# A two-layer graph network kernel: fewer copied source tiles, a second table kept on chip, node steps one group apart, one-hot matrices of 80 nodes

## The chip, the cores and the metric

One core of a Trainium2 chip runs the whole program. The metric is the device time of one execution in microseconds; the kernel before was run three times (3557.40, 3561.74 and 3564.12 us, median 3561.74 us), and once more under the profiler. "POOL" is GpSimd, "DVE" VectorE, "ACT" ScalarE, "PE" TensorE and "SP" SyncE in all that follows.

## What is computed

12,500 nodes of 128 features each, and 200,000 edges, sorted by target node. Two layers follow each other, each with a normalisation in front and a residual around it:

```python
h = relu(layernorm(x))
agg = segment_sum(h[src], dst)                       # layer 0
x = x + agg @ W_rel.T + b_rel + h @ W_root.T
h = relu(layernorm(x))
w = silu(edge_attr @ We1 + be1) @ We2 + be2          # layer 1
agg = segment_sum(h[src] * w, dst)
x = x + h + silu(agg @ Wn1 + bn1) @ Wn2 + bn2
```

What costs time is the row lookup `h[src]`: 200,000 rows of 512 bytes per layer, at indices in no order. All data are float32.

## The kernel before

**Groups and tiles.** The edges are cut into tiles of 128 and groups of 8 tiles (1,024 edges): 196 groups, 1,563 tiles per layer, the last group with three tiles. A group's eight tiles of source rows sit in one of six buffers `hs` (`HB`). The nodes are cut into 25 batches of 512 (the last of 212).

**A tile of source rows, way one: gather.** `fetch` (L241 to L257) issues one indirect DMA per tile on POOL's queue: 128 rows from HBM by a column of `src_sb`. Layer 0 reads `x` itself for the first `FG` groups (29, L134), and normalises those rows on chip (`norm`, L311); from then on it reads `h0_d`, the normalised nodes that `node_first` (L418) wrote out meanwhile, one batch per group. Layer 1 reads `h1_d`. Ahead of a group POOL waits until the group that had the buffer six groups earlier has been scattered (L244), once for the last batches of `h0_d` and once for the last two batches of `h1_d`.

**Way two: copy.** The node features of a layer also lie transposed on chip, feature by partition and node by column, in `table`. For the groups in `helped` (L67) the last tile is not gathered: DVE and ACT copy its 128 columns one by one from `table` into `hc` (`put`, L578, 128x4 bytes each; DVE takes the first 60 columns in layer 0 and 56 in layer 1, ACT the others), with the column numbers loaded into registers 16 at a time (`take`, L566); PE turns the tile back (`turn`, L608) and ACT puts it into `hs` (`place`, L614). `fetch` then issues seven gathers in place of eight. `HELP` (L35) says how many: one tile in every group of layer 0 from group 30 on, nine tiles in ten groups of layer 1 from group 26 on, each used `HW` = 4 groups after it was copied. That is 160 and 147 tiles.

**Sum by target.** For each tile DVE builds a one-hot matrix (`compare`, L259): 128 edges by `W` = 128 nodes counted from the group's first target. PE multiplies rows by one-hot (`scatter`, L368, eight matmuls into one bank), and DVE adds the window of `W` columns into `agg` (`add`, L384), where sums are kept transposed. A check on the indices sends the program to a slow second version of itself (L791 on) if some edge lies outside its group's window.

**Layer 1's edge weights.** `load` brings the edge features, `hidden` (L334) and `weigh` (L346) run both matmuls, DVE adds the bias and multiplies the rows.

**Node steps.** When the groups that can touch a batch are done, layer 0 runs `node_sum`, `node_norm`, `node_keep` and `node_store` (L452 to L501) in four successive groups: root and neighbour matmuls, moments, deviations, a clearing of that part of `agg`, normalisation, the sum that layer 1's end needs (`keep_d`), and the stores. Layer 1's table is made in its first 25 groups: `node_again` (L503) loads each batch of `h1_d` back on SP's queue, `node_turn` (L511) turns it on PE and ACT copies it into `table`, over layer 0's table. So layer 1's copied tiles start at group 26.

**Order.** All engines are programmed by hand in one static order (L745 to L784): for each group `fetch` of the next one, `compare`, the normalisation in the first groups, `add` of the group before, `scatter`, then what `plan` (L706) has put beside the group, then `spread` (the copies). Semaphores are waited for by `at` (L227), which makes the engine's own queue stand.

Of the kernel before, what the change touches and what calls it, by code (L numbers as in the profile page):

```python
# [11 lines left out]
I32 = mybir.dt.int32  # L12
# [11 lines left out]
W = 128  # L24
# [10 lines left out]
HELP = ((1, 1), (9, 10))  # L35
# [31 lines left out]
def helped(n_nodes, n_edges):  # L67

    ng = n_edges // GE
    nbt = len(last_groups(n_nodes, n_edges))
    layers = []
    for begin, (tiles, groups) in ((min(ng, nbt + FB) + 1, HELP[0]), (nbt + 1, HELP[1])):
        ends = (begin - 1 - -(i + 1) * groups // tiles for i in range(ng * tiles // groups))
        layers.append((begin, [(e + HW, e) for e in ends if e + HW < ng - 1]))
    return layers

# [12 lines left out]
def kernel(  # L92
# [41 lines left out]
    FG = min(NG, NBT + FB)  # L134
    helps = [
        (layer, h, e, begin, j)
        for layer, (begin, groups) in enumerate(helped(N, n_edges))
        for j, (h, e) in enumerate(groups)
    ]
    helped_groups = {(layer, h) for layer, h, *_ in helps}  # L140
# [17 lines left out]
    table = single([P, -(-N // P) * P], "table")  # L158
    agg = single([P, NW * WG], "agg")
    keep = table.rearrange("p (t d) -> p t d", d=D)  # L160
    table_b = table.bitcast(U8)
# [15 lines left out]
    with (  # L177
# [13 lines left out]
        hid = many(2, [P, GT * P], "hid")  # L191
        st, mv = many(2, [P, NB, 6], "st"), many(2, [P, NB, 2], "mv")
# [6 lines left out]
        help_i, = many(1, list(help_t.shape), "help_i", I32)  # L199
# [41 lines left out]
        def fetch(layer, g):  # L241

            k = layer * NG + g
            at(G, done["src", 0 if g < 8 else 1], done.get(("ap", k - (HB if g < NG - 8 else LB))))  # L244
            if layer:
                at(G, *(done["h1 out", b] for b in range(max(0, NBT - 2), NBT)))
            elif g >= FG:
                at(G, *(done["h0 out", b] for b in range(max(0, NBT - 3), NBT)))
            for t in range(tiles_of[g] - ((layer, g) in helped_groups)):
                ins = G.indirect_dma_start(  # L250
                    out=hs[k % HB][:, t, :], out_offset=None,
                    in_=h1_d if layer else x if g < FG else h0_d,
                    in_offset=bass.IndirectOffsetOnAxis(
                        ap=src_sb[:, g * GT + t : g * GT + t + 1], axis=0
                    ),
                )
                done["hs", k] = inc(ins, f"hs{k % HB}", 16)  # L257
# [12 lines left out]
        def stats(xr, n, rows, st_, mv_, sd_, free):  # L270

            at(V, *free)
            for t in range(n):
                ins = V.bn_stats(st_[:rows, t, :], xr[:rows, t, :])  # L274
            at(V, inc(ins, "dve"))
            for t in range(n):
                ins = V.bn_aggr(mv_[:rows, t, :], st_[:rows, t, :])  # L277
            at(A, inc(ins, "dve"))
            ins = A.activation(sd_[:rows, :n], mv_[:rows, :n, 1], AF.Sqrt, bias=eps[:rows])  # L279
            return inc(ins, "act")  # L280

        def scales(n, rows, mv_, sd_, rs_, nm_, deviations):
            at(V, deviations)
            ins = V.reciprocal(rs_[:rows, :n], sd_[:rows, :n])
            at(V, inc(ins, "dve"))
            ins = V.scalar_tensor_tensor(
                nm_[:rows, :n], mv_[:rows, :n, 0], -1.0, rs_[:rows, :n], op0=ALU.mult, op1=ALU.mult
            )
            return inc(ins, "dve")
# [44 lines left out]
        def hidden(g):  # L334
# [7 lines left out]
            at(A, done["hp", g], done.get(("wp", g - 2)))  # L342
# [41 lines left out]
        def add(layer, g):  # L384
# [7 lines left out]
            at(V, done["ap", k], done.get(("add", k - 1)), done["agg"])  # L392
            window = agg[:, ds(firsts[k - g % GL][g % GL], W)]
# [51 lines left out]
        def node_table(b, turned):  # L445
            n0, nt = batches[b]
            m = nt * P
            at(A, done["turned", b])
            ins = A.copy(table[:, n0 : n0 + m], turned.rearrange("p t d -> p (t d)")[:, :m])  # L449
            done["table", b] = inc(ins, "act")  # L450

        def node_sum(b):  # L452

            n0, nt = batches[b]
            at(T, done.get(("keep", b - 1)), done["const"], done["ones"], done["table", b])
            T.matmul(op[:, :nt, :], ones_r, b_rel_r[:, :nt, :], start=True, stop=False)
            for layer_agg, w_sb in ((table, w_root_sb), (agg, w_rel_sb)):
                for t in range(nt):
                    s = n0 + t * P
                    ins = T.matmul(  # L460
                        op[:, t, :], layer_agg[:, s : s + P], w_sb,
                        start=False, stop=(layer_agg is agg and t == nt - 1),
                    )
                at(T, done["add", ready[b]])
            done["op", b] = inc(ins, "pe")
            at(V, done["op", b], done["xt", b])
            o = op[:, :nt, :]
            ins = V.tensor_add(o, o, xt[b % XB][:, :nt, :])  # L468
            done["dev", b] = stats(
                op, nt, P, stn[2], mvn[2], sdn[2], (inc(ins, "dve"), done.get(("h1", b - 1)))  # L470
            )
            ins = V.memset(agg[:, n0 : n0 + nt * P], 0.0)
            done["agg"] = inc(ins, "dve")

        def node_norm(b):
            n0, nt = batches[b]
            at(A, scales(nt, P, mvn[2], sdn[2], rsn[2], nmn[2], done["dev", b]))
            if b < 2:
                at(A, *(done["h0 out", b] for b in range(max(0, NBT - 3), NBT)))
            else:  # L480
                at(A, done["h1 out", b - 2], done["keep", b - 2])
# [20 lines left out]

        def node_again(b):  # L503

            i = b % 3
            at(S, done["h1 out", b], done.get(("turned again", b - 3)))
            if b < 3:
                at(S, *(done["h1 out", c] for c in range(max(0, NBT - 2), NBT)))
            done["h1 in", b] = node_dma(b, h0[i], h1_d, f"h1in{i}", True)

        def node_turn(b):  # L511

            n0, nt = batches[b]
            at(T, done["h1 in", b], done["b3"])
            for t in range(nt):
                ins = T.transpose(op[:, t, :], h0[b % 3][:, t, :], ident)  # L516
            done["turned", b] = done["turned again", b] = inc(ins, "pe")
            at(A, done["op", NBT - 1], *done.get("columns", ()))
            node_table(b, op)
            done["b3"] = done["table", b]  # L520

        def node_hidden(b):
# [3 lines left out]
            ins = T.matmul(b3[:, :m], wn1_sb, agg[:, n0 : n0 + m], start=True, stop=True)  # L526
# [39 lines left out]
        def take(engine, chunk):  # L566
# [4 lines left out]
            _, places = nc.values_load_multi_w_load_instructions(  # L571
                help_at[i % P : i % P + 1, i // P, lo:hi], engines=[kind],
                min_val=TABLE, max_val=TABLE + 4 * (N - 1),
                skip_runtime_bounds_check_because="sources are nodes",
            )
            return chunk, places

        def put(engine, taken):  # L578

            (i, lo, hi), places = taken  # L580
            at(engine, done.get(("tile", i - 3)), *(done["table", b] for b in range(NBT)))
            for c, place_ in zip(range(lo, hi), places):
                to, column = hc_b[i % 3][:, 4 * c : 4 * c + 4], table_b[:, ds(place_ - TABLE, 4)]
# [7 lines left out]
        def spread(layer, g):  # L591
# [4 lines left out]
            for engine, rest in ((V, hooks), (A, list(chunks(layer, g, A)))):  # L596
                for chunk in rest or (chunks(layer, g, V) if engine is V and not layer else ()):
# [16 lines left out]
        def place(i, layer, h):  # L614
# [3 lines left out]
            done["hx", k] = done["placed", i] = inc(A.copy(hs[k % HB][:, GT - 1, :], bank), "act")  # L618
# [3 lines left out]
        with tc.tile_critical():  # L622
# [32 lines left out]
            done["agg"] = inc(A.copy(agg, zero.to_broadcast([P, NW * WG])), "act")  # L655
# [9 lines left out]
            ins = V.tensor_scalar(help_at, help_i, 4.0, float(TABLE), op0=ALU.mult, op1=ALU.add)  # L665
# [42 lines left out]

            for layer, parts in (
                (0, (node_sum, node_norm, node_keep, node_store)),  # L710
                (1, (node_hidden, node_out, node_out_store)),
            ):
                begin = 0 if layer else FG
                for b in range(NBT):
                    begin = max(begin, ready[b] + 1)
                    for i, part in enumerate(parts):
                        plan(layer, begin + i, lambda b=b, part=part: part(b))
                    begin += len(parts) - 1
            for b in range(min(XB, NBT)):
                plan(0, NBT + 1, lambda b=b: node_load(b))  # L720
            for b in range(NBT):
                plan(1, b - 1, lambda b=b: node_again(b))
                plan(1, b, lambda b=b: node_turn(b))
            for b in range(min(2, NBT)):
                plan(1, ready[0] - 1, lambda b=b: node_load(b, keep_d))
            for i, (layer, h, e, begin, j) in enumerate(helps):
# [6 lines left out]
                if not layer:  # L733
                    plan(0, e + 2, lambda i=i, h=h: place(i, 0, h))
            placed = {e + 1: (i, 1, h) for i, (layer, h, e, *_) in enumerate(helps) if layer}
# [8 lines left out]
            for layer in range(2):  # L744
# [5 lines left out]
                for g in range(NG):  # L750
# [3 lines left out]
                    if not layer:  # L754
                        if g + 1 < NG:
                            compared = compare(0, g + 1)
                            if not g:
                                done["oh", 1] = inc(compared, "dve")
                        if g < FG:
                            for c in range(-(-tiles_of[g] // NB)):  # L760
                                push(norm(g, c))
                            push(node_first(g) if g < NBT else nothing)
# [17 lines left out]
                    if layer and g in placed:  # L780
                        place(*placed[g])
# [193 lines left out]
```

## Time and profile before

| | |
|---|---|
| three runs | 3557.40, 3561.74, 3564.12 us |
| profiled execution | 3553.55 us |
| its span, first to last instruction | 3551.7 us |
| gathers on POOL | 2,819 (232 from `x`, 2,587 from `h0_d` or `h1_d`), 944 ns each |
| copied columns | 17,832 on DVE at 150 ns, 21,464 on ACT at 190 ns |
| one-hot builds on DVE, 128x1024 | 392, 475.0 us |
| scatter matmuls on PE, 128x128 | 6,252 records (two per tile), 1214.2 us |
| busy: PE, DVE, ACT, POOL | 64%, 71%, 74%, 75% |
| granted TensorE clock, mean | 0.753 |

Busy time counts what the profile has as an instruction's duration. Register loads, waits and the time between two DMA issues are not in it, so an engine that is shown at 75% may still be one that never rests: what tells the two apart is the list of what it waited for. "issue" as a releaser means that the engine waited for nothing that the profile shows. The profiled execution was 8.2 us below the median of the three runs, 0.2%.

### The profile page before, as it was taken

To read this page: it belongs to the slowest core of one execution; us is meant where nothing else is said; L and a number is where in the kernel's file an instruction comes from. 1 tells how busy PE (TensorE), PEld (TensorE's weight loads), DVE (VectorE), ACT (ScalarE), POOL (GpSimd) and SP (SyncE) were. 2 spreads that over 40 slices of the span, in tenths; PEclk is the share of its full clock that TensorE was granted. 3 is DMA by queue.
4 is the path that set the end of the run, shared out by engine and by line. 5 is a ranking of instruction groups with operands and counts; after the bars stand their busy time and mean duration, and the time that the engine had idled before them with its cause. 6 is when DMAs were issued, how large, how long until landed. Compare 5 with 4: busy or idle time off the path is not lost.

```text
span 3551.7 us, 73201 instructions
## 1 busy us (share of the span) xinstructions
PE 2286.8 (64%) x11405; PEld 1833.0 (52%) x11405; DVE 2510.7 (71%) x20197; ACT 2620.0 (74%) x22584; POOL 2662.7 (75%) x2826
## 2 busy tenths in 40 slices
PE   3444455445454454455567778878888788888887
PEld 3443444444444444444456566656566566566565
DVE  5555777676766767776433378888888888888885
ACT  6554888788878878887511278987888789888984
POOL 7777777777777777777677777777777777777776
PEclk7566656666666667656678888898888888988988
DMA  4332322222222222222233333332332233333322
GB/s 123 106 96 74 83 69 63 63 66 69 63 63 68 66 63 66 69 61 60 84 105 105 95 82 86 88 85 79 87 89 83 81 87 90 84 83 86 87 82 62
DMA packets 201107, 284.08 MB, mean 80 GB/s; under 512 B 49305, under 2 KB 150260, under 8 KB 195620
## 3 DMA queue, kind: packets, MB, share of 16 engines
q0 software_dynamic: 90208, 184.93, 20.0%
q1 hardware_dynamic: 110214, 94.30, 8.7%
q14 instruction: 396, 3.24, 0.3%
q8 instruction: 93, 1.52, 0.2%
q10 hardware_dynamic: 196, 0.09, 0.0%
HBM read 253.52 MB, written 25.60 MB: 79 GB/s over the span
## 4 chain that ended last, share of the span: by engine, by line
POOL 59%; issue 20%; PE 9%; DVE 5%; DMA 5%; ACT 2%; DVEq 0%; ACTq 0%; POOLq 0%; SPq 0%
POOL hs L250 59%; DMA hs<-h_d,src_sb 5%; PE bank L376 4%; PE pair L353 2%; ACT hc L587 2%; DVE hc L585 2%; DVE hs L365 2%; PE pair L340 1%; DVE pair L361 1%; PE bank L460 0%; DVE oh L263 0%; PE bank L526 0%; DVEq L571 0%; DVE xt L545 0%; ACTq L571 0%
## 5 line engine op out<-in xcount | busy, mean ns | idle before, releaser
L250 POOL DMA_INDIRECT hs<-h_d,src_sb x2587 | 2442.5, 944 | 798.5 <-issue 776.6
L587 ACT COPY hc<-table 128x4 uint8 x21464 | 2135.3, 190 | 63.3 <-issue 52.1
L376 PE MATMUL bank<-oh,hs 128*128 128x128 f32 x6252 | 1214.2, 373 | 671.7 <-DVE hs L365 300.2
L376 PEld LDWEIGHTS bank<-oh,hs 128*128 128x128 f32 x6252 | 1127.2, 279 | 885.1 <-DVE hs L365 435.4
L585 DVE TENSOR_TENSOR hc<-table,bank 128x4 uint8<-128x4 uint8 x17832 | 1303.1, 150 | 282.6 <-issue 274.7
L263 DVE TENSOR_TENSOR oh<-bank,rel 128x1024 f32<-128x1024 f32 x392 | 475.0, 1212 | 0.1
L353 PE MATMUL pair<-we_sb,hid 128*128 128x128 f32 x3126 | 428.7, 296 | 3.4 <-DVE xt L488 3.4
L361 DVE TENSOR_TENSOR pair<-pair,be_sb 128x1024 f32<-128x1024 f32 x196 | 240.2, 1226 | 261.1 <-PE pair L353 260.8
L353 PEld LDWEIGHTS pair<-we_sb,hid 128*128 128x128 f32 x3126 | 418.5, 215 | 3.5 <-DVE xt L488 3.5
L340 PE MATMUL pair<-ef,we_sb 50*128 50x512 f32 (+1 forms) x782 | 409.3, 645 | 1.2 <-ACT hid L343 1.2
L365 DVE TENSOR_TENSOR hs<-pair,hs 128x1024 f32<-128x1024 f32 x196 | 239.4, 1221 | 163.5 <-DMA hs<-h_d,src_sb 151.8
L612 PE MATMUL pair<-ident,hc 128*128 128x128 f32 x160 | 64.1, 401 | 434.6 <-ACT hc L587 277.2
L343 ACT ACTIVATE hid<-pair,be_sb 128x1024 f32<-128x1024 f32 x196 | 216.9, 1107 | 106.8 <-PE pair L340 106.3
L250 POOL DMA_INDIRECT hs<-in_x,src_sb x232 | 219.0, 944 | 71.2 <-issue 70.4
L612 PEld LDWEIGHTS pair<-ident,hc 128*128 128x128 f32 x160 | 28.7, 180 | 460.1 <-issue 141.1
L340 PEld LDWEIGHTS pair<-ef,we_sb 50*128 50x128 f32 x782 | 135.0, 192 | 132.7 <-issue 120.2
L279 ACT ACTIVATE sdn<-mvn,eps 128x4 f32<-128x4 f32 (+1 forms) x50 | 14.5, 289 | 247.0 <-DVE mvn L277 247.0
L449 ACT COPY table<-bank 128x512 f32<-128x512 f32 (+1 forms) x25 | 14.4, 577 | 176.2 <-PE bank L516 176.2
L528 ACT ACTIVATE hid<-bank,bn_sb 128x512 f32<-128x512 f32 (+1 forms) x25 | 17.0, 678 | 153.9 <-PE bank L526 153.9
L274 DVE BATCH_NORM_STATS2 st<-hs 128x6 f32<-128x128 f32 x232 | 50.3, 279 | 111.2 <-DMA hs<-in_x,src_sb 111.2
L394 DVE TENSOR_TENSOR agg<-agg,bank 128x128 f32 x392 | 109.2, 279 | 27.0 <-PE bank L376 19.7
L468 DVE TENSOR_TENSOR bank<-bank,xt 128x512 f32<-128x512 f32 (+1 forms) x25 | 17.2, 688 | 149.4 <-PE bank L460 149.4
(68 smaller groups left out, 910.4 us busy)
## 6 DMA issues: line engine op xcount, KB each, us to landing
hs<-h_d,src_sb POOLq DMA_INDIRECT x2587
ef<-in_ef_t SPq DMA_DIRECT2D x98, 408.0 KB
xt<-in_x SPq DMA_DIRECT2D x48, 256.0 KB, 3.9
h_d<-h SPq DMA_DIRECT2D x48, 256.0 KB, 2.5
keep_d<-xt SPq DMA_DIRECT2D x24, 256.0 KB, 2.4
h<-h_d SPq DMA_DIRECT2D x24, 256.0 KB, 5.3
xt<-keep_d SPq DMA_DIRECT2D x24, 256.0 KB, 10.0
out_x<-xt SPq DMA_DIRECT2D x24, 256.0 KB, 2.7
```

The lines of the kernel that those rows point to most:

```text
L250: ins = G.indirect_dma_start(out=hs[k % HB][:, t, :], out_offset=None, in_=h1_d if layer else x if g < FG else h0_d, in_offset=bass.Indire ...
L263: return V.tensor_tensor(oh[k % OB][:, :n, :], io.unsqueeze(1).to_broadcast([P, n, W]), rel[:, g, :n].unsqueeze(2).to_broadcast([P, n, W]) ...
L340: ins = T.matmul(hp_b[:, c : c + m], we1_sb, e[:, c : c + m], start=True, stop=True)
L343: ins = A.activation(hid[g % 2][:, :n], hp_b[:, :n], AF.Silu, bias=be1_sb)
L353: ins = T.matmul(wp[:, t, :], hid[g % 2][:, t * P : (t + 1) * P], we2_sb, start=True, stop=True)
L361: ins = V.tensor_add(w, w, be2_sb.unsqueeze(1).to_broadcast([P, n, D]))
L365: done["msg", g] = inc(V.tensor_mul(h, w, h), "dve")
L376: ins = T.matmul(ap[k % AB], hs[k % HB][:, t, :], oh[k % OB][:, t, :], start=(t == 0), stop=(t == tiles_of[g] - 1),)
L394: done["add", k] = inc(V.tensor_add(window, window, ap[k % AB]), "dve")
L585: ins = V.tensor_tensor(to, column, zero_b, ALU.bitwise_or)
L587: ins = A.copy(to, column)
L612: done["tile", i] = inc(T.transpose(bank, hc[i % 3], ident), "pe")
```

## The change

- `HELP` becomes three tiles in four groups in layer 0 and three in five in layer 1. Layer 0's copies begin at group 18 (`FG` is 17 now) and layer 1's at group 1. The number of tiles is 129 and 113.
- `node_first` runs twice per group, so layer 0's table and `h0_d` are complete after 13 groups in place of 25.
- `table` and `agg` become two halves of one tensor that change roles: layer 0 has its table in the first half and its sums in the second; each batch, once normalised, is turned on PE and copied by ACT over its own sums (`node_turn`, `node_send`), where it is layer 1's table. Layer 1 sums into the first half, which is cleared by four ACT copies in groups 191 to 194 and two DVE memsets. `node_again`, with its loads of `h1_d`, is gone.
- The node steps of layer 0 are seven, each planned one group after the one it waits for; near the layer's end they are drawn together by a factor of three.
- `W` is 80: one-hot matrices, scatter matmuls and window adds are 80 nodes wide.
- In layer 0 the first register load for DVE's copies is taken right after `compare`.

```diff
-W = 128
+W = 80
-HELP = ((1, 1), (9, 10))
+HELP = ((3, 4), (3, 5))
...
-    for begin, (tiles, groups) in ((min(ng, nbt + FB) + 1, HELP[0]), (nbt + 1, HELP[1])):
+    for begin, (tiles, groups) in ((min(ng, -(-nbt // 2) + FB) + 1, HELP[0]), (1, HELP[1])):
...
-    FG = min(NG, NBT + FB)
+    FG = min(NG, -(-NBT // 2) + FB)
...
+    both = single([P, 2 * NW * WG], "both")
+    halves = both[:, : NW * WG], both[:, NW * WG :]
+    agg = halves[1]
...
-            for t in range(tiles_of[g] - ((layer, g) in helped_groups)):
+            for t in range(tiles_of[g] - helped_groups.count((layer, g))):
...
-            at(T, done.get(("keep", b - 1)), done["const"], done["ones"], done["table", b])
+            at(T, done.get(("sent", b - 1)), done["const"], done["ones"], done["table", b])
...
-            ins = V.memset(agg[:, n0 : n0 + nt * P], 0.0)
-            done["agg"] = inc(ins, "dve")
+            if b >= cleared:
+                at(V, done["op", b], *done.get("columns", ()))
+                ins = V.memset(halves[0][:, n0 : n0 + WG], 0.0)
+                done["sums", 1].append(inc(ins, "dve"))
+
+        def clear(b0, b1):
+
+            at(A, done["op", b1 - 1], *done.get("columns", ()))
+            s0, s1 = b0 * WG, b1 * WG
+            ins = A.copy(halves[0][:, s0:s1], zero.to_broadcast([P, s1 - s0]))
+            done["sums", 1].append(inc(ins, "act"))
...
-            done["h1 in", b] = node_dma(b, h0[i], h1_d, f"h1in{i}", True)
...
-            at(T, done["h1 in", b], done["b3"])
+            at(T, done["h1", b], done["keep", b])
             for t in range(nt):
-                ins = T.transpose(op[:, t, :], h0[b % 3][:, t, :], ident)
+                ins = T.transpose(op[:, t, :], h1[b % 2][:, t, :], ident)
+            done["h1 turned", b] = inc(ins, "pe")
+
+        def node_send(b):
+            n0, nt = batches[b]
+            at(A, done["h1 turned", b])
+            ins = A.copy(halves[1][:, n0 : n0 + nt * P], b3[:, : nt * P])
+            done["sent", b] = done["b3"] = inc(ins, "act")
...
-                (0, (node_sum, node_norm, node_keep, node_store)),
+                (0, (
+                    (0, node_sum), (1, node_moments), (2, node_deviations), (3, node_scales),
+                    (4, node_norm), (5, node_keep), (5, node_store), (5, node_turn), (6, node_send),
+                )),
...
+                        if not layer and begin > NG - 9:
+                            i //= 3
...
+                        hooks.extend(chunks(0, g, V))
                         if g + 1 < NG:
                             compared = compare(0, g + 1)
+                            hook()
...
                         if g < FG:
+                            if 2 * g < NBT:
+                                push(node_first(2 * g))
                             for c in range(-(-tiles_of[g] // NB)):
                                 push(norm(g, c))
-                            push(node_first(g) if g < NBT else nothing)
+                            push(node_first(2 * g + 1) if 2 * g + 1 < NBT else nothing)
```

## The prediction

> **What bounds the kernel now.** I read the page's busy shares and its chain first, then what POOL waited for, then the work by stage. The shares do not name a bound: four engines are between 64% and 75%. The chain does.
>
> ```profile
> ## 4 chain that ended last, share of the span: by engine, by line
> POOL 59%; issue 20%; PE 9%; DVE 5%; DMA 5%; ACT 2%; DVEq 0%; ACTq 0%; POOLq 0%; SPq 0%
> ```
>
> POOL's gathers and the "issue" time between them are 79% of it. Whether POOL is the bound all the way is decided by its waits:
>
> ```profile
> POOL hs L250 <- issue: 847.0, 2779, 0.3
> POOL hs L250 <- DMA h_d<-h: 10.3, 1, 10.3
> POOL hs L250 <- PE pair L340: 3.4, 11, 0.3
> POOL hs L250 <- PE bank L376: 2.7, 9, 0.3
> ```
>
> The columns are total us, times, longest. The 0.3 us before a gather is there 2,779 times for nothing visible, and the few that carry a name are no longer: this is the price of one gather after another, not a wait. One wait of 10.3 us, at the switch of layers, is the only time that POOL stands for others. So 2,819 gathers go out one after another, and the end comes when the last is done. Their pace, from the timeline: layer 1's first gather starts at 1766.10 us and its last, the 1,416th, at 3532.49, so 1766.39 / 1415 = 1.248 us each (944 ns busy, 0.30 between). Layer 0, 4.47 to 1754.86 in 1,401 steps, gives 1.249. The sum 1,403 x 1.249 + 10.0 + 1,416 x 1.248, with 3.1 us ahead and 18.3 us behind (3533.4 to 3551.7), is 3551 us, which is the span.
>
> Does this pace depend on what the other engines do? The work by stage answers it, a stretch without copies against one with them:
>
> ```profile
> core 0: us, PE busy (x) PEld busy (x) DVE busy (x) ACT busy (x) POOL busy (x), PEclk, DMA share, GB/s
> ...
> 1800.00:1900.00 100.00, 75.95 (x412) 59.38 (x412) 38.46 (x41) 17.16 (x21) 75.62 (x81) 0.82 0.40 108
> ...
> 2400.00:2800.00 400.00, 330.30 (x1735) 246.91 (x1734) 332.59 (x2451) 343.00 (x3008) 302.23 (x321) 0.87 0.30 84
> ```
>
> DVE goes from 38% to 83%, ACT from 17% to 86%, DMA from 40% to 30%, and POOL is at 75.6% in both. It neither waits for DVE and ACT nor is slowed by them.
>
> **The change, part by part.**
>
> *Number of copied tiles.* In the built programs POOL issues 2,819 gathers before and 2,884 after (136 from `x`, 2,748 from `h0_d` and `h1_d`). The earlier starts add groups to the copying, and the lower rates take more away: 160 + 147 = 307 tiles become 129 + 113 = 242. 65 more gathers x 1.2486 us = +81.2 us, all of it on the path, as POOL has no idle time to put them in.
>
> *Copies saved.* DVE loses 17,832 - (129x60 + 113x56 = 14,068) = 3,764 columns x 150 ns = 565 us, ACT 21,464 - 16,908 = 4,556 x 190 ns = 866 us. By the stage rows above this is beside POOL: 0. One rule speaks for a gain: the Trainium skill, "SBUF — State Buffer", in its warning on DVE blocking a DMA, says that DVE instructions in a two-port mode lock GpSimd out of writing descriptors. If each copy held POOL for its 150 ns, up to 565 us would come back. The row disagrees: 2,451 DVE instructions per 400 us against 41 per 100 leave POOL's share equal to 0.06 points, so at most 0.08% of the span, 3 us; I take 0. (The page names one-input instructions outside that mode as harmless; no row here shows the mode.)
>
> *One-hot of 80 nodes.* The builds of 128x384 took 0.49 and 0.55 us, those of 128x1024 1.21, so about 0.78 for 640: 392 x 0.43 = 169 us less on DVE, and PE and the window adds shrink too. Beside POOL: 0, except at the two ends, where the last scatter (0.94 and 0.83 us) and the window add (0.28) lie on the path. Between nothing and five eighths, some 0.3 to 0.5 us at each: I take -0.8 in all. The inputs' widest group reaches 71 nodes past its first target, so no edge falls out of a window of 80, and the slow version does not run.
>
> *Tables sooner.* Each of the first 13 groups gets a second batch on DVE and ACT. In the stretch from 50 to 250 us, 20 groups, ACT is busy 66.2 + 11.6 us with rows and 32.9 + 11.2 + 5.6 with batches: 3.9 + 2.5 = 6.4 us per group. A second batch makes it 8.9, and POOL's pace gives 8 x 1.249 = 9.99. So ACT has 1.1 us to spare where it had 3.6. What covers a shortfall: the new wait, for `h0_d` before group 17, comes at 3 + 136 x 1.249 = 173 us. The 25th batch belongs to group 12, whose rows land by some 135 us; with a group's work and the store (2.5 us to landing) it is out by about 150. The slack is some 23 us over 13 groups, so POOL waits only if a group takes over 11.8 us. Queued behind that wait are all of layer 0's gathers from group 17. Bounds: 0; and, if ACT's waits for DVE's moments (83.3 us in these 20 groups, 4.2 each) stayed whole, 13.1 us a group and 13 x 3.1 - 23 = 17 us. I take 0: those waits sit in time that was spare, and shrink when more is queued.
>
> *Table of layer 1 from layer 0.* 25 loads leave SP's queue and 98 turns and 25 copies (0.58 us) move from layer 1 to layer 0. No gather waits for any of it: 0. Each is planned after what it needs, so PE, which stands for `keep` at a turn with the next `scatter` behind it, finds it done; POOL would notice only a PE six groups (50 to 60 us) late, three in the last eight groups.
>
> *Node steps a group apart.* ACT's 247.0 us of waiting for moments (17.0 at most) and DVE's 149.4 for `node_sum` go away. They hide behind POOL: 0. It matters at the switch of layers, where the last batch has no later group:
>
> ```profile
> 1754.86 0.94 POOL L250 DMA_INDIRECT hs<-h_d,src_sb  x1 [0.30 <-issue]
> ...
> 1760.57 0.43 DVE L468 TENSOR_TENSOR bank<-bank,xt 128x256 f32<-128x256 f32 x1 [1.33 <-PE bank L460]
> ...
> 1763.40 0.34 SPq L411 DMA_DIRECT2D h_d<-h  x1
> ...
> 1766.10 0.94 POOL L250 DMA_INDIRECT hs<-h_d,src_sb  x1 [10.30 <-DMA h_d<-h]
> ```
>
> Landing, scatter, add, sum, moments, sqrt, scales, normalisation, store and its landing are the same steps after: 10 us stay. The DVE memset in it is 512 wide in place of 256 (0.48 for 0.27, partly beside the sqrt): +0.1. The batch before is done earlier, and had not been what ended last.
>
> *Early register load in layer 0, clearing by ACT* (four copies, 12,800 columns took 10.86 us, so about 10 in all): hidden by the same cover, 0.
>
> **Sum.** +81.2 - 0.8 + 0.1 = +80.5 us. On the profiled execution, 3553.55 + 80.5 = 3634; on the median of the runs, 8.2 us higher, 3642. I predict for the median: 3642 us, 2.3% slower.
>
> **Rivals.**
> 1. *POOL waits as well.* ACT falls behind in the first 13 groups and the wait at group 17 shows, or PE is held at a turn near the end of layer 0, where only three buffers cover it. For: ACT at 8.9 of 10.0 us, and a turn holds PE for a normalisation (1.50), a sum (0.68) and the turn (0.60) if nothing was ahead, 3 us for each of the last two batches. Against: 23 us of slack. Up to 17 + 6 = 23 us more: 3643 to 3665, say 3655. Chance 0.12.
> 2. *Faster: POOL is freed.* DVE's copies do hold back the descriptors, in the copying stages of both layers. Each gather must become 81 / 2884 = 28 ns quicker before this pays; at the lock's full price, 565 us, the time would be 3642 - 565 = 3077, and it decides from a seventh of that price. Against: the equal shares above. Chance 0.02.
> 3. *No difference: the copies were the bound.* ACT at 86% with register loads on top would set the pace, POOL's 0.3 us would be back-pressure, and the lighter load would pay for the gathers: 3562. Against: the same 0.3 us at 1800 to 1900 us, where nothing is copied, and at the very start. Chance 0.02.
>
> That leaves 0.84 for the forecast. A measurement of this kernel can tell about 0.2% from no change. Slower by over 0.2%: 0.84 + 0.12 = 0.96; within: 0.02; faster: 0.02. The range: the profiled execution and the runs span 3553.55 to 3564.12, which with +80.5 is 3634 to 3645; 5 us below for a pace that is 1.6 ns quicker per gather, and up to the first rival's 3665. So 3629 to 3665.
>
> **What would show it.** In the profile after: 2,884 gathers at 944 ns with 0.30 between, POOL's busy share still 75 to 77% in every slice, a span near 3632. DVE busy near 49% ((2510.7 - 565 - 169) / 3632) and ACT near 48% ((2620.0 - 866) / 3632), with no gain from it. One wait of about 10 us at the switch; a second one, before the first gather from `h0_d`, would be the first rival. A gather mean below 916 ns or gaps below 0.27 us would be the second. It is wrong if POOL's idle time has another named releaser, or if the pace differs from 1.248 us.

## The result

The changed kernel took 3652.64 us (median of four runs, 3647.13 to 3652.77), the kernel before 3561.46 us (3557.40 to 3564.12): a ratio of 1.0253, with a 95% interval of 1.0235 to 1.0271. The difference is 91.2 us where 80.5 was predicted. The profiled execution took 3652.66 us, its span is 3650.9 us.

The chain that ended last, after:

```profile
## 4 chain that ended last, share of the span: by engine, by line
POOL 64%; issue 21%; PE 9%; DMA 3%; DVE 2%; ACT 0%; DVEq 0%; ACTq 0%; POOLq 0%; SPq 0%
```

POOL and the time between its gathers are 85% of it now, 79% before. What POOL waited for (total us, times, longest):

```profile
POOL hs L267 <- issue: 868.9, 2850, 0.3
POOL hs L267 <- DMA h_d<-h: 15.7, 1, 15.7
POOL hs L267 <- PE bank L400: 4.0, 13, 0.3
```

The picture is that of before, with one wait, at the switch, and that one is 5.4 us longer. The groups of gathers, by the tensor that they read, and the work by stage:

```profile
L267 POOL DMA_INDIRECT hs<-h_d,src_sb x2748 | 2599.8, 946 | 853.2 <-issue 827.7 <-DMA h_d<-h 15.7 <-PE bank L400 4.0
L267 POOL DMA_INDIRECT hs<-in_x,src_sb x136 | 128.8, 947 | 42.1 <-issue 41.2 <-DMA src_sb<-in_src_t 1.0
```

```profile
core 0: us, PE busy (x) PEld busy (x) DVE busy (x) ACT busy (x) POOL busy (x), PEclk, DMA share, GB/s
...
2400.00:2800.00 400.00, 348.35 (x1661) 271.71 (x1662) 249.22 (x1656) 238.91 (x1936) 302.43 (x321) 0.77 0.31 84
```

DVE fell from 332.6 to 249.2 us of these 400 and ACT from 343.0 to 238.9, and POOL's busy time is 302.4 in place of 302.2: it got nothing from that. In the last columns TensorE's granted clock is 0.77 where it was 0.87.

**Where 99.2 us of span went.** By POOL's gathers in the timeline, 65 more of them x 1.248 us are 81.1. The pace in this profiled execution is 1.2504 us and not 1.2483, which over 2,884 gathers is 6.0; it is not the change's (it goes from run to run, below). The switch is 15.73 for 10.30, +5.4. The end, from the start of the last gather (3625.26 us) to the end of the span, is 25.6 for 19.2, +6.4. With +0.1 at the start the sum is 99.0. The medians of the runs differ by 91.2: 81.2 for the count, and 10.0 that are left for the switch and the end, where the two profiles have 11.8. Which pace those other runs had is not on record.

The switch after, to be read against the four lines of before:

```profile
1796.66 0.95 POOL L267 DMA_INDIRECT hs<-h_d,src_sb  x1 [0.30 <-issue]
1796.99 0.30 ACT L299 ACTIVATE sdn<-mvn,eps 128x4 f32<-128x4 f32 x1 [21.96 <-DVE mvn L294]
...
1797.20 2.73 ACT L508 COPY both<-zero 128x3072 f32<-128x3072 f32 x1
...
1799.84 1.50 ACT L317 ACTIVATE h<-bank,nmn,rsn 128x128 f32<-128x128 f32 x4
...
1802.17 0.71 PEld L549 LDWEIGHTS bank<-ident,h 128*128 128x128 f32 x4 [3.28 <-ACT h L317]
...
1803.08 1.41 PE L400 MATMUL bank<-oh,hs 128*128 128x80 f32 x6
...
1807.77 0.43 DVE L497 TENSOR_TENSOR bank<-bank,xt 128x256 f32<-128x256 f32 x1 [2.90 <-PE bank L486]
...
1810.65 0.34 SPq L435 DMA_DIRECT2D h_d<-h  x1
...
1813.35 0.95 POOL L267 DMA_INDIRECT hs<-h_d,src_sb  x1 [15.73 <-DMA h_d<-h]
```

The last gather ends at 1797.6. The batch before the last is then still being normalised, and on ACT a clearing copy (L508, 2.73 us) stands ahead of its normalisation (L317), whose scales are ready at 1798.2: an estimate of 1.65 us lost (1799.84 - 1798.19). PE waits at the turn (L549) for the normalisation and for DVE's sum behind it (L530), with the last scatter (L400) queued behind, which starts 5.5 us after the last gather's end, where before it was 2.1 (1755.80 to 1757.88):

```profile
1757.88 0.94 PE L376 MATMUL bank<-oh,hs 128*128 128x128 f32 x6 [0.59 <-DMA hs<-h_d,src_sb]
```

From scatter to the sum with `xt` it is 4.7 us for 2.7, at a granted clock of 0.50 from 1780 to 1800 us and also from 1795 to 1811 us; before, it was 0.85 from 1752 to 1764 us.

The end, before and after, with one pair of matmuls that the change left alone (L536, now L573) and the last scatter:

```profile
3532.49 0.94 POOL L250 DMA_INDIRECT hs<-h_d,src_sb  x1 [0.30 <-issue]
...
3535.34 1.12 PE L536 MATMUL bank<-bn_r,ones_r 1*128 1x512 f32 x2
...
3537.38 0.83 PE L376 MATMUL bank<-oh,hs 128*128 128x128 f32 x6
```

```profile
3625.26 0.94 POOL L267 DMA_INDIRECT hs<-h_d,src_sb  x1 [0.30 <-issue]
...
3629.82 2.07 PE L573 MATMUL bank<-bn_r,ones_r 1*128 1x512 f32 x2
...
3633.69 1.41 PE L400 MATMUL bank<-oh,hs 128*128 128x80 f32 x6
```

The granted clock is 0.96 from 3532 to 3543 us before and 0.55 from 3625 to 3641 us after.

In four of the six sets of runs below (e1, e2, e3, e5; e6; e8 to e11; e13) every kernel, the one before too, ran about a third longer than elsewhere (before: 4846 to 4919 us), with engines idle for long stretches whose releaser the profile does not name, so no time of theirs is compared with one from elsewhere.

### The profile page after: what moved, and what is told of

Its sections match the earlier page's. It is cut to its first block, busy times and chain, and to the rows that moved or that the text cites. A ratio compares the mean times of both kernels' runs of the same rounds, so it can differ in the third digit from the quotient of the medians.

```text
span 3650.9 us, 63584 instructions
## 1 busy us (share of the span) xinstructions
PE 2470.2 (68%) x11340; PEld 2018.1 (55%) x11340; DVE 2016.8 (55%) x16171; ACT 2157.3 (59%) x17847; POOL 2729.9 (75%) x2891
## 4 chain that ended last, share of the span: by engine, by line
POOL 64%; issue 21%; PE 9%; DMA 3%; DVE 2%; ACT 0%; DVEq 0%; ACTq 0%; POOLq 0%; SPq 0%
POOL hs L267 64%; PE bank L400 4%; PE pair L377 3%; DMA hs<-h_d,src_sb 3%; PE pair L364 1%; DVE hs L389 1%; DVE pair L385 1%; PE bank L563 0%; PE bank L573 0%; PE bank L575 0%; PE bank L486 0%; DVE xt L582 0%; ACT hc L626 0%; PE bank L651 0%; PE bank L482 0%
## 5 line engine op out<-in xcount | busy, mean ns | idle before, releaser
L267 POOL DMA_INDIRECT hs<-h_d,src_sb x2748 | 2599.8, 946 | 853.2 <-issue 827.7
L400 PE MATMUL bank<-oh,hs 128*128 128x80 f32 x6252 | 1245.9, 381 | 1095.2 <-DMA hs<-h_d,src_sb 795.3
L400 PEld LDWEIGHTS bank<-oh,hs 128*128 128x128 f32 x6252 | 1171.0, 288 | 1318.3 <-DMA hs<-h_d,src_sb 844.2
L626 ACT COPY hc<-both 128x4 uint8 x16908 | 1680.6, 189 | 135.7 <-issue 129.3
L624 DVE TENSOR_TENSOR hc<-both,bank 128x4 uint8<-128x4 uint8 x14068 | 1026.7, 149 | 165.0 <-issue 162.9
L377 PE MATMUL pair<-we_sb,hid 128*128 128x128 f32 x3126 | 552.8, 350 | 0.0
L377 PEld LDWEIGHTS pair<-we_sb,hid 128*128 128x128 f32 x3126 | 530.3, 264 | 0.0
L418 DVE TENSOR_TENSOR both<-both,bank 128x80 f32 x392 | 91.5, 233 | 515.1 <-PE bank L400 503.9
L280 DVE TENSOR_TENSOR oh<-bank,rel 128x640 f32<-128x640 f32 x392 | 318.4, 812 | 0.0
L267 POOL DMA_INDIRECT hs<-in_x,src_sb x136 | 128.8, 947 | 42.1 <-issue 41.2
L555 ACT COPY both<-bank 128x512 f32<-128x512 f32 (+1 forms) x25 | 14.4, 578 | 93.7 <-PE bank L549 93.7
L486 PEld LDWEIGHTS bank<-w_root_sb,both 128*128 128x128 f32 x196 | 43.7, 327 | 36.7 <-issue 36.7
```

Of the source, the lines that this page charges most:

```text
L267: ins = G.indirect_dma_start(out=hs[k % HB][:, t, :], out_offset=None, in_=h1_d if layer else x if g < FG else h0_d, in_offset=bass.Indire ...
L280: return V.tensor_tensor(oh[k % OB][:, :n, :], io.unsqueeze(1).to_broadcast([P, n, W]), rel[:, g, :n].unsqueeze(2).to_broadcast([P, n, W]) ...
L377: ins = T.matmul(wp[:, t, :], hid[g % 2][:, t * P : (t + 1) * P], we2_sb, start=True, stop=True)
L400: ins = T.matmul(ap[k % AB], hs[k % HB][:, t, :], oh[k % OB][:, t, :], start=(t == 0), stop=(t == tiles_of[g] - 1),)
L418: done["add", k] = inc(V.tensor_add(window, window, ap[k % AB]), "dve")
L624: ins = V.tensor_tensor(to, column, zero_b, ALU.bitwise_or)
```

## The experiments

### The rates alone on the kernel before (e12; e2 and e9)

```diff
--- before
-HELP = ((1, 1), (9, 10))
+HELP = ((3, 4), (3, 5))
```

> The kernel before with the new rates alone, its copying starts and all else unchanged: 2,908 gathers, 89 more than before. Theory: +89 x 1.249 = +111, 3673 us, with the wait at the switch near 10.3 us and the time from the last gather's start to the end near 19.2 us, as before. Rival (the copies held POOL back, so fewer of them pay back): clearly under 3660 us. Rival (the 10 us beyond the count come with the lower rates): the switch and the end are 5 us longer each, 3683 us.

Measured: 3674.42 us against 3563.21, +111.2 us, ratio 1.0307 (1.0290 to 1.0324). 89 gathers were expected to cost 111, so the price of one is 1.25 us, on this code too. Both rivals fall. The waits of POOL:

```profile
POOL hs L250 <- issue: 874.2, 2867, 0.3
POOL hs L250 <- DMA h_d<-h: 10.6, 1, 10.6
```

The switch stays at 10.6 us, so what lengthened it comes from another part of the change. The end is 22.7 us in this execution, with the old code and 128 nodes: 3.5 us longer than before (why, under e7).

The same kernel in e2 and e9:

> The kernel before with the new rates alone, its copying starts unchanged: 2,908 gathers, 89 more than before. Theory: +89 x 1.249 = +111, 3672 us, with the wait at the switch still near 10.3 us and the time from the last gather's start to the end still near 19.2 us. Rival (the copies held POOL, so fewer of them pay back): clearly under 3660 us. Rival (the 10 us beyond the count come with the lower rates): the switch and the end are 5 us longer each here too, 3683 us.

> The kernel before with the new rates alone, its copying starts unchanged: 2,908 gathers, 89 more than before. Theory: +89 x 1.249 = +111, 3673 us, with the wait at the switch near 10.3 us and the time from the last gather's start to the end near 19.2 us, as before. Rival (the copies held POOL, so fewer of them pay back): clearly under 3660 us. Rival (the 11 us beyond the count come with the lower rates): the switch and the end are 5 us longer each, 3683 us.

4715.01 us against 4915.03 for the kernel before beside it, and 4725.56 against 4919.45: 4% faster, where 3% slower was expected. The same kernel there is not bound by POOL alone, which in e2 stands for scatters:

```profile
POOL hs L250 <- PE bank L376: 681.5, 133, 22.4
```

So these two say nothing on the price of a gather where POOL never rests. They do say that fewer copied tiles can pay where it does rest; what held the engines up in these runs is open.

### One-hot matrices of 128 nodes again (e7; e3)

```diff
--- after
-W = 80
+W = 128
```

> The changed kernel with one-hot matrices of 128 nodes again, repeated some hours after e3. 2,884 gathers. If the narrow one-hot is what lowered TensorE's granted clock and so lengthened the switch (15.7 us against 10.3) and the end (25.6 against 19.2), the clock returns to about 0.75, the switch to 11 or 12 us, the end to about 19.5 us: 3641 to 3645 us. If the order of the node steps is what lengthened them, clock and time stay as changed, 3652 us.

Measured: 3647.47 us against 3562.62, ratio 1.0241 (1.0224 to 1.0258), so 84.9 us over before where the changed kernel has 91.2. The median lies between the two expectations, with two runs at 3645 and two at 3650, and the two intervals overlap: by the times alone the 6.3 us are not clear of noise. The clock is. The same stages of both kernels, changed first:

```profile
600.00:1600.00 1000.00, 499.81 (x2164) 445.99 (x2163) 506.86 (x5349) 610.39 (x5775) 756.35 (x800) 0.52 0.25 65
2000.00:3400.00 1400.00, 1204.50 (x5763) 937.61 (x5763) 865.45 (x5711) 836.88 (x6778) 1058.70 (x1120) 0.78 0.31 83
```

And with 128 nodes:

```profile
600.00:1600.00 1000.00, 475.87 (x2164) 423.27 (x2163) 556.19 (x5342) 613.22 (x5775) 756.18 (x800) 0.64 0.23 65
2000.00:3400.00 1400.00, 1087.70 (x5774) 831.27 (x5773) 933.95 (x5697) 841.38 (x6793) 1058.78 (x1120) 0.86 0.29 83
```

The first two pairs are PE's matmuls and weight loads, the number behind POOL's pair is the granted clock. The same 2,164 matmuls take PE 24 us more when the one-hot is narrower, at a clock of 0.52 in place of 0.64. All four runs of the changed kernel have 0.65 to 0.69, all four with 128 nodes 0.74 to 0.75. The switch:

```profile
1794.89 2.74 ACT L508 COPY both<-zero 128x3072 f32<-128x3072 f32 x1
...
1797.53 1.50 ACT L317 ACTIVATE h<-bank,nmn,rsn 128x128 f32<-128x128 f32 x4
...
1800.37 0.83 PE L400 MATMUL bank<-oh,hs 128*128 128x128 f32 x6
...
1810.47 0.95 POOL L267 DMA_INDIRECT hs<-h_d,src_sb  x1 [12.34 <-DMA h_d<-h]
```

12.3 us and not 15.7; the end is 19.9 (from 3622.97 us on) and not 25.6. So 9 of the 11.8 us at the two ends are gone in this execution. The end goes with the clock that it meets: 0.96 before (19.2 us long), 0.97 here from 3622 to 3633 us (19.9), 0.55 in the changed kernel (25.6). In e12, with 128 nodes, it is 0.57 from 3650 to 3658 us and 1.00 from there to 3664 (22.7). So the wide one-hot can meet a low clock at the end too, and how often is not known; some of the 5.7 us may be chance.

At the switch the last scatter starts 2.2 us after the last gather's end (1798.13), as before: with the clock up, the sum of the batch before the last takes PE 3.1 us (1789.47 to 1792.58) and not 5.8 (1789.10 to 1794.88), and its turn is out of the way in time, in spite of the clearing copy. The 2.0 us that stay come after the scatter. The last sum waits until ACT has copied the turned batch out of their common bank (L555), and its last eight matmuls (L486, 0.71 + 0.61 us before) find a slower clock (0.65 from 1802 to 1805 us):

```profile
1802.21 0.69 PE L482 MATMUL bank<-b_rel_r,ones_r 1*128 1x256 f32 x2 [1.01 <-ACT both L555]
...
1802.83 1.19 PE L486 MATMUL bank<-w_root_sb,both 128*128 128x128 f32 x4
...
1803.81 1.06 PE L486 MATMUL bank<-w_rel_sb,both 128*128 128x128 f32 x4
```

> The changed kernel with one-hot matrices of 128 nodes again: 2,884 gathers. If the narrow one-hot is what lowered TensorE's granted clock (0.65 to 0.69 against 0.75) and so lengthened the switch (15.7 us against 10.3) and the end (25.6 against 19.2), the clock returns to about 0.75 in the mean, the switch to 11 or 12 us, the end to about 19.5 us, and the time is 3641 to 3645 us in spite of more work on DVE and PE. If the order of the node steps is what lengthened them, clock and time stay as changed, 3652 us, or a little over.

In e3 it took 4727.96 us against 4915.03 for the kernel before, with POOL standing 580.8 us for scatters (L400), which leaves no reading of the width.

### No copied tiles at all (e10; e5)

```diff
--- after
-HELP = ((3, 4), (3, 5))
+HELP = ((1, 400), (1, 400))
```

> The changed kernel with no copied tiles at all: 3,126 gathers, 242 more than changed, no column copied by DVE or ACT. Theory (POOL's pace does not depend on the copies): 3652 + 242 x 1.25 = 3955 us, 944 to 947 ns per gather and 0.30 us between. Rival (copies hold POOL): the pace falls below 1.23 us and the time is under 3900 us.

> The changed kernel with no copied tiles at all: 3,126 gathers, 242 more than changed, no column copied by DVE or ACT. Theory (POOL's pace does not depend on the copies): 3652 + 242 x 1.25 = 3955 us, 944 to 947 ns per gather and 0.30 us between. Rival (copies hold POOL): the pace falls below 1.23 us and the time is under 3900 us.

They took 4854.05 us against 4919.45 for the kernel before, and 4825.67 against 4915.03. In e10 POOL stands 639.7 us for scatters (L400), so the 3955 us are not tested. The gathers themselves can be read. e10, without one copied column:

```profile
L267 POOL DMA_INDIRECT hs<-h_d,src_sb x2990: 938/944/2220, 207.9 to 4816.4; - x200
```

(duration in ns, least / median / most), and e13 below, with 342 copied tiles:

```profile
L267 POOL DMA_INDIRECT hs<-h_d,src_sb x2648: 938/944/2221, 205.8 to 4801.6; - x190
```

The intervals from one gather to the next without a wait (under 1.3 us) have a mean of 1.2481 us in both. So 43,776 columns copied by DVE and ACT change a gather by nothing that shows in the nanosecond. The rival in which copies hold POOL back falls, as far as a gather's own time goes, and so does the one in which the 0.3 us between gathers are back-pressure from the copies: they are there without a single copy.

### The old rates on the changed kernel (e8; e1 and e6)

```diff
--- after
-HELP = ((3, 4), (3, 5))
+HELP = ((1, 1), (9, 10))
```

> The changed kernel with the old rates of copied tiles (one in every group, nine in ten groups) and all the rest of the change: 2,784 gathers, 100 fewer than changed, 35 fewer than before. Theory (each gather is 1.25 us on the path; switch and end about 11 us longer than before): 3562 - 44 + 11 = 3529 us, so the sign of the change turns round. Rival (with 342 tiles to copy DVE and ACT set the pace): POOL shows named waits in the copying stages and the time is over 3545 us. Rival (copies hold POOL back): a gather's mean rises over 950 ns and the time is over 3545 us.

> The changed kernel with the old rates of copied tiles (one per group, nine in ten groups) and all the rest of the change: 2,784 gathers, 100 fewer than changed, 35 fewer than before. Theory (each gather is 1.25 us on the path, the rest of the change costs about 11 us at the switch of layers and at the end): 3561 - 44 + 11 = 3528 us, so the sign of the change turns round. Rival (with 342 tiles to copy DVE and ACT set the pace): POOL shows named waits over 0.3 us in the copying stages and the time is over 3545 us. Rival (fewer copies free POOL, so more copies slow it): a gather's mean rises over 950 ns and the time is over 3545 us.

> The changed kernel with the old rates of copied tiles, on another chip than the run named e1[...] (before: 4915 us). 2,784 gathers. Theory (each gather is 1.25 us on the path, the rest of the change costs some 11 us at the switch and the end): 3561 - 44 + 11 = 3528 us. Rival (with 342 tiles to copy DVE and ACT set the pace): POOL shows named waits in the copying stages and the time is over 3545 us. If all is held up here too (before over 3600 us), neither can be read.

4940.62 us against 4919.45 for the kernel before, 4943.16 against 4915.03, 4939.36 against 4908.93: within 0.8% of it each time. In e8 POOL stands 1159.6 us for scatters (L400), but it does so without any copies too (e10), so neither side is decided.

### Old rates, 128 nodes, later clearing (e13; e11)

```diff
--- after
-W = 80
+W = 128
-HELP = ((3, 4), (3, 5))
+HELP = ((1, 1), (9, 10))
...
-                    plan(0, NG - 5 + i, lambda b0=b0, b1=b1: clear(b0, b1))
+                    plan(0, NG - 5 + i if i < 2 else NG, lambda b0=b0, b1=b1: clear(b0, b1))
```

> The changed kernel with the old rates of copied tiles, one-hot matrices of 128 nodes, and the last two of the four clearing copies moved behind the last node steps: 2,784 gathers, 35 fewer than before. Theory: -35 x 1.249 = -44 us; with 128 nodes the end is as before (19 us); the switch loses the 2.7 us that a clearing copy put ahead of a normalisation, and is 1 to 2 us longer than before's 10.3: 3563 - 44 + 2 = 3521 us, faster than both kernels. Rival (342 tiles and the wide one-hot are too much for the groups' 8.7 to 8.9 us): named waits on POOL in the copying stages, over 3545 us.

> The changed kernel with the old rates, one-hot matrices of 128 nodes, and the last two of the four clearing copies moved behind the last node steps: 2,784 gathers. Theory: 35 fewer gathers than before are -44 us; with 128 nodes the end is as before (19 us); the switch loses the 2.7 us that the clearing copy put ahead of the last normalisation but one, and stays 1 to 3 us longer than before's 10.3: 3562 - 44 + 2 = 3520 us. Rival (342 tiles and the wider one-hot on DVE are too much for the groups' 8.7 to 8.9 us): named waits on POOL, over 3545 us.

4829.46 us against 4845.92 for the kernel before (ratio 0.9984, 0.9959 to 1.0008) and 4928.08 against 4919.45, with POOL standing 1087.7 us for scatters in e13. Whether 2,784 gathers beat both kernels, as 35 x 1.25 = 44 us off the count would have it, stays open: it needs DVE and ACT to keep up with 342 tiles, and no run shows that where POOL is the bound. What the later clearing is worth at the switch stays open with it.

## Why the prediction was right, and where it was not

- *The bound and the count.* Right. 65 gathers at 1.25 us are 81.2 of the 91.2 us, and e12 gives the same price for 89 of them by the rates alone.
- *The range.* 3652.64 us is above the forecast's own 3634 to 3645 and lies in the range only by the room that was kept for the first rival. Of that rival's two waits the one before group 17 did not come; a turn near the end of layer 0 did hold PE, at the switch. So the cause and the size of the count were right, and that the other 10 us still fell inside is in part luck.
- *Copies saved: 0.* Right for the time. The Trainium skill's warning on DVE blocking a DMA ("SBUF — State Buffer") would have brought up to 565 us by the prediction's estimate, had it applied to these copies; e10 and e13 show no part of it. But the sizes were misread: 3,764 columns x 150 ns is not the busy time saved. Copies overlap in their engine, so a group's busy time is less than count times mean. DVE's group went from 1303.1 to 1026.7 us, 276 less and not 565, ACT's from 2135.3 to 1680.6, 455 less and not 866. Hence DVE at 55% and ACT at 59%, where 49 and 48 were announced. Nothing hung on it.
- *One-hot of 80 nodes: -0.8 us.* The term that missed most. With e7 beside it, the narrow one-hot cost about 9 us in the profiled executions (3.4 at the switch, 5.7 at the end, of which some may be chance) and 6.3 by the difference to before in the runs (91.2 - 84.9), which is within their noise. That the saving failed is plain; that the cost is 6 to 9 us rests on one profile of each. The step said that the last scatter and the window add get 0.3 to 0.5 us shorter at each end, in proportion to the columns (80 of 128 is three eighths less). The add did, from 0.28 to 0.23; the scatter went from 0.94 to 1.41 us at the switch and from 0.83 to 1.41 at the end. The group before and after:

```profile
L376 PE MATMUL bank<-oh,hs 128*128 128x128 f32 x6252 | 1214.2, 373 | 671.7 <-DVE hs L365 300.2
L400 PE MATMUL bank<-oh,hs 128*128 128x80 f32 x6252 | 1245.9, 381 | 1095.2 <-DMA hs<-h_d,src_sb 795.3
L400 PEld LDWEIGHTS bank<-oh,hs 128*128 128x128 f32 x6252 | 1171.0, 288 | 1318.3 <-DMA hs<-h_d,src_sb 844.2
```

  Before, the weight loads had 279 ns in the mean. A matmul takes 421 ns in the median at either width: the 128x128 rows are the weights here, their load takes 333 ns in the median at either width, and only the quickest matmuls show the change (235 ns for 274). And the clock fell, to 0.50 at the switch and 0.55 at the end. The Trainium skill, "TensorE: Matmul & The Clock Gate", in its part on the clock gate, says that the array runs at half rate unless it has been kept busy; the 0.50 at the switch is such a half rate. By that rule a shorter moving matrix is a risk where PE works in bursts, which the prediction did not weigh; no run here shows how the chip counts busy.
- *Tables sooner: 0, bound 17.* Right. No wait stands ahead of the first gather from `h0_d`.
- *Layer 1's table from layer 0, node steps a group apart: 0, and 10 us at the switch.* Off POOL's path they cost nothing, as said. At the switch the step "the same steps after" failed: it left out that the last sum shares a bank with the turned batch before it (`done["sent", b - 1]` in the diff), which is 1.0 us in e7, and that a late turn holds the last scatter, as it did at the low clock. The first rival had named the turn, at 3 us a batch.
- *Clearing by ACT: 0, hidden.* Not at the switch: there a clearing copy holds a normalisation for an estimated 1.65 us. In e7 the same copy held nothing that mattered, so here it cost only where the turn was late anyway.
- *The level.* The median was to be 8 us over the profiled execution. Here it was equal (3652.64 and 3652.66). The profiled execution of before had the quick pace, 1.2483 us, and that of after the slow one, 1.2504. Why the fourth run of after is 5.5 us quicker than the other three is open: the quick pace would make 2.1 ns x 2,884 = 6.1, a short end 5.7. In e7 the quickest of four runs (3644.69 us, the others up to 3649.86) had the slow pace, 1.2508, and a short end.

## What to carry to other kernels

When one queue issues the same instruction from start to end without waiting, count those instructions and multiply by their pace: the rest of a large change is worth what it does to the few places where that queue stands. Here relief on engines that the queue does not wait for bought nothing, and work moved back to the queue was paid in full. Look at those places again for every step that the change queues ahead of them, and for the clock at which they run.

## What the runs showed of the hardware

A narrower moving matrix lowered TensorE's granted clock, with as many matmuls as before: 0.52 for 0.64 in layer 0, 0.78 for 0.86 in layer 1 (e7 beside the changed kernel; the mean clocks of all four runs of each part the same way), and PE was busier for less arithmetic. And the pace of indirect DMAs has two values, 1.2481 to 1.2483 us (944 ns each) and 1.2504 to 1.2508 (946 or 947), constant within an execution to 0.0006 us from one stretch of 350 gathers to the next. One and the same kernel shows both (e6 1.2481, e1 and e8 1.2507), so it isn't the program that chooses. What does is open; over 2,900 gathers it is 6 us.
